# Four graph layers over 32 batches: first two batches and the last turn's last layer in halves, bias rows spread by a product, two batches kept on chip

## The chip, the cores and the metric

The kernel runs on one core of one Trainium2 chip. The metric is the time on the device in microseconds (us); a run's time is that of one launch. Times of single instructions come from one profiled execution of the kernel. In what follows PE is the matrix engine (TensorE) and PEld its loading of stationary operands, DVE is VectorE, ACT is ScalarE, POOL is GpSimd and SP is SyncE, which here only issues transfers. L1234 is line 1234 of the kernel before.

## What is computed

32 batches of a graph with 512 nodes and 128 features each, `x` (32, 512, 128), and a symmetric adjacency `adj` (32, 512, 512) of zeros and ones go through four residual layers. Every layer first takes a layer norm and a ReLU of x.

```python
h = relu(ln(x)); x = x + attention(h, adj)     # q, k, v = relu(h W + b); softmax over the neighbours; times v
h = relu(ln(x)); x = x + gcn_lstm(h, adj)      # sigmoid((A_norm h) @ lw); lw: a 3-tap convolution of the
                                               # last 128 nodes, then an LSTM of 128 steps over all batches
h = relu(ln(x)); x = x + four_layers(h, adj)   # each: tanh of ((src and dst sums over normalized adj), own) @ wu + bu,
                                               # with inputs of 1, 1, 2 and 3 blocks of 128 features
h = relu(ln(x)); x = x + prelu(adj @ (h W^T) + bias)
```

## The kernel before

Two programs stand in the kernel. `symmetric` makes the whole result if the adjacency is symmetric and the exponentials stay in range; it counts violations as it goes, and at its end each engine loads a flag and branches past `general`, which would compute everything again without those assumptions.

`symmetric` does not issue its instructions as it meets them. Each piece of work is an operation with an engine (or a choice of ACT or DVE), an estimated duration, a rank and the tiles it reads and writes. `Plan.run` (L613 to L791) simulates the engines with these estimates, takes the operation of lowest rank that can start first, and so writes an order for every engine. On the chip each engine then works through its order strictly, and waits on semaphores where its input is late. The constants at L537 to L541 and L811 to L832 feed this planner: `SWITCH` is the time it assumes for a change between whole products and products in 32-column tiles, `FIRST_GAPS`, `LANDED` and `STORED` are the times it assumes for transfers to land, `PATIENCE` and `LEAD` shift what goes first.

The work has these stages:

- Head (L959 to L987): ACT issues the loads of the attention weights, of the column biases `colb` and of the row bias R_V, broadcast to all partitions into `brow`. It then loads its function table. SP's first loads are x of the first batches. PE runs 20 warm-up products on a tile of zeros (`warm_up`, L981).
- Pass 1 (`pass_1`, L1164) goes over all batches; position 0 is the first batch that is not in `RESIDENT` (L822), and the resident batches 0, 1 and 2 come last. For each it loads x and the last 128 columns of the adjacency (`f_al`), normalizes, transposes (L902, or L1198), makes keys (`f_pk`), the query of the last 128 nodes (`f_pql`) and values (`f_pv`), and the attention of those nodes (`f_sl`, `f_pol`), which the convolution (`f_pd`) and the LSTM need. Only position 0 works in halves of two tiles each (L1182 to L1203). The value product adds to a PSUM bank that `fill` (L992) has filled with the bias. A batch that is not resident stores its keys and relu'd inputs (448 KB) and values (258 KB). The folding of the weights of the third layer's source, own and target products (`fold`, L1030) is spread among positions 2 to 5 (`FOLD_AT`).
- Pass 2 (`pass_2`, L1361) finishes the attention of the other 384 nodes, in products of 32 columns (`f_pq`, `f_s`, `f_po`), from the stored or resident tiles. The LSTM (`lstm`, L1289) runs its 128 steps through it with the highest priority.
- The rest (`rest`, L1556) is done in 32 turns, one batch each, several in flight. A turn makes the gate, then the four layers (L1640 to L1663). Each layer is a product `f_py` into a bank filled with the bias, a split of the result into a rounded part and a remainder (L1501 on ACT, L1502 on DVE), the sums over neighbours `f_pa` (8 products of 512 columns), a scaling by `f_inv` (L1654 on DVE), the own products added to the same bank (L1658), and a tanh (L1662 on ACT). After the fourth layer its result is transposed back (`f_n4T`), added to x (L1679) and normalized; then come the products with the adjacency (`f_pg`), an eviction to `f_g`, the last matrix (`f_p`, L1706) and the update: L1709 adds the positive part, L1713 and L1714 the negative one. For turns 29 and 30 L1713 and L1714 are put off behind the last turn's normalization (`put_off`, L1530).
- The last turn (turn 31): its normalization is `relu_first` (L1514): statistics of four tiles, one root on POOL (L1091), the shift, then scaling and rounding on ACT (L1525) and the remainder on DVE (L1527). The products with the adjacency run in two column halves (L1693). 16 warm-up products are interspersed (L1677). The second half's store is issued by ACT, the first's by SP (L1719). The flag's load (`read`, L1752) comes after that.

## Time and profile before

| | us |
|---|---|
| median of 3 runs | 1277.38 (1276.59 to 1277.43) |
| profiled execution, its time | 1275.34 |
| profiled execution, its span from first to last instruction | 1273.4 |
| PE busy, DVE busy, ACT busy, POOL busy | 1255.8, 985.9, 837.8, 400.7 |
| first product of the LSTM (`f_z`) | 190 |
| last product of the last turn's fourth layer | 1249.9 to 1252.6 |
| issue of the last store | 1266.87 |

The page gives busy times, but PE's busy time contains warm-up products and matmuls whose ends are modelled; an engine that is busy for 99% may still lose time to both. The chain of waits lists, in order of time, what the end depended on; its pieces are not stretched, so the work of a stretch can be summed from it. The view of stretches gives each engine's busy time in a window, with the share of the 16 DMA engines. In a timeline row the numbers are start, busy time, engine, line, operation, output from inputs and count; the brackets hold the idle time before it and what released it.

### The profile page before, as it was taken

Reading aid. Unit: us, or ns where it says so; the run is one execution under the profiler, and the core shown is the slowest. Engines: PE = TensorE matmul, PEld = TensorE weight load, DVE = VectorE, ACT = ScalarE, POOL = GpSimd, SP = SyncE. Lnnn points to the kernel's source line nnn. Section 1 sums busy time; section 2 is a strip of 40 time slices with the busy share of each in tenths; the row PEclk is TensorE's granted clock in tenths of the full one; section 3 lists DMA queues with packets and bytes.
Section 4 is the critical chain, followed back from the end, with each engine's and each line's share of the span. In section 5 each row is a group of like instructions: output and inputs, shape, how many; then the busy total and the mean of one; then the engine's idle time right before and its main releaser. Section 6 shows DMA issues by size and latency. Waiting matters only on the chain.

```text
span 1273.4 us, 33089 instructions
## 1 busy us (share of the span) xinstructions
PE 1255.8 (99%) x12074; PEld 970.9 (76%) x12075; DVE 985.9 (77%) x3275; ACT 837.8 (66%) x2102; POOL 400.7 (31%) x734
## 2 busy tenths in 40 slices
PE   9999999999999999999999999999999999999997
PEld 7988876666666767777778787787787877877775
DVE  7899869989899889775677677676776776787755
ACT  4667677778777667774576676666766766675433
POOL 3556533324233135331223233232242232332001
PEclk9999999999999999999999999999999999999999
DMA  8888887778986797876476677777777777482211
GB/s 270 255 274 277 275 270 233 213 226 272 277 259 214 213 251 210 174 175 160 83 178 156 155 173 160 153 174 152 175 154 151 175 157 153 89 174 59 50 33 37
DMA packets 313052, 232.02 MB, mean 182 GB/s; under 512 B 151601, under 2 KB 258481, under 8 KB 312881
## 3 DMA queue, kind: packets, MB, share of 16 engines
q1 hardware_dynamic: 295280, 212.65, 61.5%
q0 software_dynamic: 16896, 16.78, 8.5%
q8 instruction: 97, 1.59, 0.5%
q14 instruction: 75, 0.61, 0.2%
q10 hardware_dynamic: 704, 0.40, 0.1%
HBM read 135.73 MB, written 62.58 MB: 156 GB/s over the span
## 4 chain that ended last, share of the span: by engine, by line
PE 86%; DVE 6%; POOL 2%; ACT 2%; DMA 2%; issue 1%; SPq 0%; ACTq 0%; DVEq 0%
PE f_pa L1538 18%; PE f_py L1647 15%; PE f_pa L1658 15%; PE f_pg L1538 8%; PE f_po L1415 5%; PE f_z L1303 4%; PE f_s L1409 4%; PE f_pol L1251 2%; PE f_pk L1177 2%; PE f_p L1706 2%; PE f_sl L1241 2%; PE f_pv L1219 2%; PE f_pl L1612 2%; PE f_pd L1276 2%; PE f_pq L1399 1%; DVE f_e L1413 1%
## 5 line engine op out<-in xcount | busy, mean ns | idle before, releaser
L1538 PE MATMUL f_pa<-f_ar,f_y 128*128 128x512 f32 x1024 | 298.0, 428 | 0.2 <-ACT f_y L1501 0.2
L1538 PEld LDWEIGHTS f_pa<-f_ar,f_y 128*128 128x128 f32 x1024 | 189.3, 188 | 73.1 <-issue 38.7
L1647 PE MATMUL f_py<-f_wf,f_n 128*128 128x128 f32 x1280 | 173.7, 275 | 0.0
L1647 PEld LDWEIGHTS f_py<-f_wf,f_n 128*128 128x128 f32 x1280 | 165.0, 191 | 10.1 <-issue 2.9
L1662 ACT ACTIVATE f_n<-f_pa,f_bcol 128x512 f32<-128x512 f32 x128 | 88.3, 690 | 101.9 <-PE f_pa L1658 99.0
L1658 PE MATMUL f_pa<-f_n,f_wf 128*128 128x512 f32 x320 | 152.7, 593 | 0.1
L1456 ACT ACTIVATE f_ar<-f_a 128x512 fp32r<-128x512 f32 x224 | 138.7, 622 | 4.1 <-PE f_pg L1538 2.4
L1463 POOL DMA_DIRECT2D f_das<-f_ar x32 | 27.1, 846 | 360.2 <-ACT f_ar L1456 338.1
L1501 ACT CAST f_y<-f_py 128x512 fp32r<-128x512 f32 x128 | 75.3, 589 | 72.1 <-PE f_py L1647 65.5
L1502 DVE TENSOR_TENSOR f_y<-f_py,f_y 128x512 fp32r<-128x512 f32 x128 | 87.7, 687 | 34.9 <-ACT f_y L1501 33.4
L1654 DVE TENSOR_TENSOR f_pa<-f_pa,f_inv 128x512 f32<-128x512 f32 x128 | 86.9, 694 | 28.0 <-PE f_pa L1538 27.9
L1415 PE MATMUL f_po<-f_v,f_e 128*32 128x129 f32 x3072 | 108.0, 273 | 0.4 <-DVE f_e L1413 0.2
L1415 PEld LDWEIGHTS f_po<-f_v,f_e 128*32 128x32 f32 x3072 | 90.9, 110 | 21.1 <-issue 16.6
L1658 PEld LDWEIGHTS f_pa<-f_n,f_wf 128*128 128x128 f32 x320 | 57.9, 190 | 47.0 <-issue 42.6
L1409 PE MATMUL f_s<-f_q,f_k 128*32 128x384 f32 x928 | 92.0, 486 | 0.2 <-issue 0.2
L1303 PE MATMUL f_z<-f_w,f_seq 128*32 128x128 f32 x2040 | 83.4, 276 | 5.2 <-DVE f_seq L1349 2.3
L1303 PEld LDWEIGHTS f_z<-f_w,f_seq 128*32 128x32 f32 x2040 | 53.0, 109 | 45.1 <-ACT f_e L1412 10.0
L1132 DVE COPY f_hl_d<-f_n 128x1024 uint16<-128x1024 uint16 x27 | 18.7, 694 | 88.0 <-ACT f_n L1662 88.0
L1472 DVE SCALAR_TENSOR_TENSOR f_aT<-f_a,f_aT 128x1024 bf16<-128x1024 f32 (+1 forms) x68 | 76.3, 1152 | 0.5 <-DMA f_aT<-f_das 0.5
L1647 PE MATMUL f_py<-f_wf,f_T_c 128*128 128x128 f32 x448 | 72.8, 275 | 0.0
L1538 PE MATMUL f_pg<-f_ar,f_xp_d 128*128 128x512 f32 x248 | 71.9, 413 | 0.0
L1538 PE MATMUL f_pg<-f_ar,f_xp_c 128*128 128x512 f32 x256 | 68.4, 407 | 0.6 <-ACT f_xp_c L1509 0.4
(213 smaller groups left out, 2755.1 us busy)
## 6 DMA issues: line engine op xcount, KB each, us to landing
f_a<-in_adj_dram SPq DMA_DIRECT2D x112, 256.0 KB
f_a<-in_adj_dram SPq DMA_DIRECT2D x28, 1024.0 KB
f_das<-f_ar POOLq DMA_DIRECT2D x32, 512.0 KB, 4.8
f_dkq<-f_kh SPq DMA_DIRECT2D x29, 448.0 KB
f_al<-in_adj_dram SPq DMA_DIRECT2D x32, 256.0 KB
f_inv<-f_ddi SPq DMA_DIRECT2D x32, 256.0 KB
f_x<-in_x_dram SPq DMA_DIRECT2D x31, 256.0 KB
out_dram<-f_x SPq DMA_DIRECT2D x31, 256.0 KB
```

Of the source, the lines that this page charges most:

```text
L1303: nc.tensor.matmul(z.t[part, k, :, :], h, w[:, m : m + 4, part], start=False, stop=True, skip_group_check=True)
L1409: PE(R, t_mm(NR), lambda s=s, j=j: quarters(lambda p: nc.tensor.matmul(s.t[p], keys_of()[:, j * P + p.start : j * P + p.stop], q_of(), sta ...
L1415: PE(R, t_mm(P), lambda e=e, t=t, j=j: quarters(lambda p: nc.tensor.matmul(po.t[p, t, :], e.t[:, t * P + p.start : t * P + p.stop], v.t[:, ...
L1456: ACT(rank, 0.62, lambda t=t: nc.scalar.activation(ar.t[:, t, :], a.t[:, t, :], AF.Square, accum_out=deg.t[:, t : t + 1]), [(a, t)], [(ar, ...
L1472: nc.vector.scalar_tensor_tensor(flat(aT.t[:, n * k : n * (k + 1), :]), flat(a.t[:, n * k : n * (k + 1), :]), 1.0, flat(aT.t[:, n * k : n ...
L1501: ACT(rank, t_act(N), lambda: nc.scalar.copy(parts.t[:, :, 0, :], src.t), [src], [(parts, 0)])
L1502: DVE(rank, t_dve(N), lambda: nc.vector.tensor_sub(parts.t[:, :, 1, :], src.t, f32(parts.t[:, :, 0, :])), [src, (parts, 0)], [(parts, 1)])
L1538: nc.tensor.matmul(pg.t, parts.t[:, j, k, :], ar.t[:, j, :], start=(k == 0 and j == 0), stop=(k == 1 and j == NT - 1))
L1647: nc.tensor.matmul(py.t[:, j, :], nodes[n].t[:, bass.ts(j, P)], wf[:, W_F[i] + c, 0, :], start=False, stop=(c == nch - 1), skip_group_chec ...
L1654: before = DVE(R, t_dve(N), lambda pa=pa: nc.vector.tensor_mul(pa.t, pa.t, inv_row.t), [inv_row], [pa])
L1658: nc.tensor.matmul(pa.t, wf[:, W_F[i] + c, 1, :], nodes[n].t, start=False, stop=(c == nch - 1), skip_group_check=True)
L1662: ACT(R, 0.57, lambda pa=pa, n=n, i=i: nc.scalar.activation(n.t, pa.t, AF.Tanh, bias=bcol[:, i : i + 1]), [pa], [n])
```

## The change

The parts, in the order of the program:

1. Constants of the planner: `SWITCH`, `FIRST_GAPS`, `LEAD`, `STORED`, `PATIENCE`, `FOLD_AT`; one operation (the flag's load) gets an earlier rank.
2. `RESIDENT` is two batches, not three.
3. Loads of the head: column biases first, then the function table, then the attention weights. The rows R_V and R_CONV are loaded as one row into partition 0 of a zeroed 128 x 256 tile (part of the LSTM's sequence tile), and a product with a matrix of ones spreads them to all partitions; ACT copies them out. The two broadcast loads go. The convolution's weights are loaded later. 17 warm-ups, not 20.
4. Pass 1: x of the first three positions is loaded ahead of the rest; positions 0 and 1 (`HALVED` = 2) work in halves of two tiles; position 0's fill with the value bias is for ACT only.
5. The last turn: the fourth layer (`BY_HALVES` = (3,)) by halves of two tiles (`layer_by_halves`), the transposing back and adding by halves (`update_by_halves`), the normalization's statistics and root by halves (`relu_first`); 4 + 3 warm-ups, not 16.
6. L1709 of a put-off turn is put off too; for turn 30 (`WAITING`) it waits for the last turn's remainders; L1713 comes after L1709.
7. The flag is loaded after the last eviction of `f_g`, not after the last store's issue.

```diff
-    SWITCH = (0.28, 0.1)
+    SWITCH = (0.25, 0.12)
...
-                first = self.lead if sub == 4 else 0.0
+                first = self.lead if sub == 4 else 60.0 if sub == 3 else 0.0
...
-    FOLD_AT = (2, 3, 4, 5)
+    FOLD_AT = (3, 4, 5, 6)
...
-    RESIDENT = range(3)
-    FIRST_GAPS = (2.0, 2.8, 3.0, 3.5)
-    LEAD = 0.0
+    RESIDENT = range(2)
+    FIRST_GAPS = (2.0, 3.5, 4.0, 4.0)
+    LEAD = 3.0
...
-    STORED = 3.0
-    PATIENCE = 1.3
+    STORED = 3.5
+    PATIENCE = 1.1
...
-    load_beside(w[:, :W_CONV, :], weights[:, :W_CONV, :], w_att, 3.5)
     load_beside(colb, cols, w_cols, 3.0)
-    load_beside(brow[:, BR_V, :], rows[R_V].partition_broadcast(P), (biases, BR_V), 3.0)
     ACT(HEAD, 1.5, lambda: nc.scalar.activation(table, neg_half[:, 0, 0:1], AF.Exp))
-    w_conv = load(HEAD + 12, 192, w[:, W_CONV:W_IH, :], weights[:, W_CONV:W_IH, :])
-    w_crow = load(HEAD + 12, 64, conv_row, rows[R_CONV].partition_broadcast(P))
+    load_beside(w[:, :W_CONV, :], weights[:, :W_CONV, :], w_att, 3.0)
+    two_rows = flat(seq[:, : 2 * P // B, :])
+    nc.vector.memset(two_rows, 0.0)
+    w_rows = plan.fixed(two_rows)
+    load_beside(two_rows[0:1], rows[R_V : R_CONV + 1].rearrange("(o r) f -> o (r f)", o=1), w_rows, 2.5)
+    w_conv = load(HEAD + 22, 192, w[:, W_CONV:W_IH, :], weights[:, W_CONV:W_IH, :])
+    w_crow = plan.fixed(conv_row)
...
-    for k in range(20):
+    for k in range(17):
...
+    spread = bank("f_spread", (P, 2, P), whole=False)
+    PE(HEAD, t_mm(2 * P), lambda: nc.tensor.matmul(flat(spread.t), ones, two_rows, start=True, stop=True), [w_rows], [spread])
+    ACT(HEAD, t_act(P), lambda: nc.scalar.copy(brow[:, BR_V, :], spread.t[:, 0, :]), [spread], [(biases, BR_V)])
+    ACT(HEAD + 11, t_act(P), lambda: nc.scalar.copy(conv_row, spread.t[:, 1, :]), [spread], [w_crow])
...
-        n = 2 if pos == 0 else NT
+        n = 2 if pos < HALVED else NT
...
-            DMA(R, 64 * n, lambda at=at: nc.sync.dma_start(xc.t[:, at : at + n, :], ...
+            DMA(R if pos > 2 else HEAD + pos, 64 * n, lambda at=at: nc.sync.dma_start(xc.t[:, at : at + n, :], ...
...
-        fill(R, lambda: pv.t, bias(BR_V), [(biases, BR_V)], pv, [turned])
+        fill(R, lambda: pv.t, bias(BR_V), [(biases, BR_V)], pv, [turned], pos == 0)
...
     def relu_first(rank, xc, name):
+        for at in range(0, NT, HALF):
+            tiles = range(at, at + HALF)
+            mv = ln_stats(rank, xc, tiles, f"{name}_{at}")
+            ln_rstd(rank, mv, at, at + HALF, (lambda rs=rs, at=at: rs.t[:, at : at + HALF], rs), True)
+            for t in tiles:
+                DVE(rank, t_dve(P), lambda t=t, mv=mv: nc.vector.tensor_scalar(y.t[:, t, :], ...
...
+    def layer_by_halves(R, b, i, nodes, ar, inv_row, before):
...
+        for at in range(0, NT, HALF):
+            cols = slice(at * P, (at + HALF) * P)
+            pa = bank(f"f_pa_{b}_{i}_{at}", (P, HALF * P), whole=False)
+            for k in range(2):
+                for half in range(0, NT, HALF):
+                    def quarter(pa=pa, cols=cols, k=k, half=half):
+                        for j in range(half, half + HALF):
+                            nc.tensor.matmul(pa.t, parts.t[:, j, k, :], ar.t[:, j, cols], ...
...
+            before = DVE(R, t_dve(HALF * P), lambda pa=pa, cols=cols: nc.vector.tensor_mul(pa.t, pa.t, inv_row.t[:, cols]), ...
+            PE(R, nch * t_mm(HALF * P), own, [nodes[m] for m in CHUNKS[i]], [pa])
+            ACT(R, t_act(HALF * P) + 0.1, lambda pa=pa, cols=cols: nc.scalar.activation(n.t[:, cols], pa.t, AF.Tanh, ...
...
+            if turn == B - 1 and i in BY_HALVES:
+                before = layer_by_halves(R + 4, b, i, nodes, ar, inv_row, before)
+                continue
...
-            for k in range(2 * BUFS["mm"]):
+            for k in range(4 if two else 7):
                 warm_up(R - 4, 0.216, f"f_warm_{k}_{b}", [end4])
...
-            evict(R, n * P, lambda cols=cols: g3.t[:, cols], lambda p3a=p3a: p3a.t, [p3a], [(g3, at)])
+            late.append(evict(R, n * P, lambda cols=cols: g3.t[:, cols], lambda p3a=p3a: p3a.t, [p3a], [(g3, at)]))
+            for k in range(3 if at else 0):
+                warm_up(R - 4, 0.216, f"f_warm_{k}_{at}_{b}", [agg3])
...
+                up = DVE(R, t_dve(n * P), lambda: nc.vector.scalar_tensor_tensor(
+                    flat(xc.t[:, part, :]), flat(p3.t), 0.0, ...), [p3], mine, after=split if turn in WAITING else ())
-                ACT(R, t_act(n * P), lambda: nc.scalar.activation(neg.t[:, part, :], p3.t, AF.Relu, scale=-1.0), [p3], [(neg, at)], after=turned)
+                ACT(R, t_act(n * P), lambda: nc.scalar.activation(neg.t[:, part, :], p3.t, AF.Relu, scale=-1.0), [p3], [(neg, at)], after=list(turned) + [up])
...
-        PE(R + 4, 0.1, read, [], [], after=[said] + late)
+        PE(R + 3, 0.1, read, [], [], after=[said] + late)
```

## The prediction

> **What bounds the kernel now.** I read the page's busy table first, then the busy time by stretch, then the two ends in order of time.
>
> ```profile
> PE 1255.8 (99%) x12074; PEld 970.9 (76%) x12075; DVE 985.9 (77%) x3275; ACT 837.8 (66%) x2102; POOL 400.7 (31%) x734
> ...
> 0.00:7.45 7.45, 6.26 (x21) 2.51 (x21) 3.40 (x19) 1.49 (x2) 2.51 (x14) 1.00 0.71 181
> 7.45:14.02 6.57, 5.01 (x35) 3.92 (x33) 5.37 (x25) 3.14 (x8) 1.78 (x3) 1.00 0.94 311
> ...
> 14.00:190.00 176.00, 175.26 (x1496) 153.59 (x1496) 148.80 (x652) 119.26 (x257) 92.11 (x232) 1.00 0.85 273
> 190.00:515.00 325.00, 318.76 (x6460) 225.63 (x6461) 292.19 (x1205) 241.59 (x845) 108.23 (x193) 1.00 0.82 236
> 515.00:1254.50 739.50, 739.08 (x3995) 576.25 (x3994) 525.57 (x1346) 465.66 (x977) 195.03 (x292) 1.00 0.64 139
> 1254.50:1267.30 12.80, 11.45 (x73) 8.97 (x72) 10.55 (x31) 6.66 (x16) 1.07 (x1) 1.00 0.21 63
> ```
>
> A row holds the stretch, its length, then busy time of PE, PEld, DVE, ACT and POOL, clock, DMA share and GB/s. From 14 to 1254.5 us PE is busy for 1233.1 of 1240.5 us. The time is therefore PE's work, which the change leaves almost as it is, plus what PE loses. It loses a head, a few us in the LSTM stretch (6.2), and a tail. PE busy flatters both ends, because warm-up products count as busy. The head, in order of time:
>
> ```profile
> 1.19 6.42 PE L984 MATMUL f_warm<-f_marks 128*128 128x512 bf16 x20 [1.19 <-DVE f_marks L922]
> ...
> 5.96 0.60 DVE L1192 TENSOR_SCALAR f_xn_a<-f_x,f_mv_a,f_rs_a 128x128 f32<-128x128 f32 x2 [0.21 <-POOL f_rs_a L1091]
> ...
> 7.45 0.60 PE L1198 MATMUL f_xt_a<-f_ident,f_xn_a 128*128 128x128 f32 x4
> ...
> 8.39 0.69 DVE L1004 COPY f_pv<-f_brow 128x512 f32<-128x512 f32 x1
> ...
> 10.70 0.48 DVE L1081 BATCH_NORM_STATS2 f_st_a<-f_x 128x6 f32<-128x128 f32 x2 [1.17 <-DMA f_x<-in_x_dram]
> ...
> 11.71 1.13 PE L1241 MATMUL f_sl<-f_ql,f_kh 128*128 128x128 f32 x8 [0.75 <-DVE f_sh_a L1112]
> ```
>
> The first two normalized tiles are there at 6.56, but PE's queue still holds warm-ups and the transposes start at 7.45. Later DVE stands 1.17 us for the third batch's x (issued at 4.39, landed at 10.67 by the chain of waits), and the eviction of the second half of the first batch's keys (L1180 at 11.10) is queued behind it, so the scores wait. Real work in 7.45 to 14.02, by the chain's spacings, is transposes 0.44, keys 0.86, query 0.22, values 0.89, scores 0.89, second batch's transposes 0.44, a weight's transposes 0.33: 4.07 of 6.57 us. PE gives away 2.5 us there and the whole 7.45 before. The tail:
>
> ```profile
> 1255.22 0.60 PE L902 MATMUL f_n4T<-f_ident,f_n 128*128 128x128 f32 x4
> ...
> 1256.59 0.68 DVE L1679 SCALAR_TENSOR_TENSOR f_x<-f_n4T,f_x 128x512 f32<-128x512 f32 x1
> ...
> 1258.86 1.07 POOL L1091 TENSOR_TENSOR f_rs_d<-f_rs_d,f_neg_half 128x4 f32<-128x4 f32 x1 [6.30 <-ACT f_p L1000]
> ...
> 1260.35 0.69 DVE L1709 SCALAR_TENSOR_TENSOR f_x<-f_p,f_x 128x512 f32<-128x512 f32 x1 [0.39 <-PE f_p L1706]
> ...
> 1260.96 1.13 DVE L1527 SCALAR_TENSOR_TENSOR f_xp_d<-f_yr_d,f_rs_d,f_xp_d 128x128 fp32r<-128x128 f32 x4
> ```
>
> The last turn's tanh ends at 1253.37 and its first product of the last layer (L1693) starts at 1260.75: 7.4 us of transposing, adding, statistics, root and relu. The chain of waits shows what PE did meanwhile that is no work: f_warm pieces of 0.59, 0.86, 0.23, 0.23 and 1.09 us, 3.0 in all. After the last store each engine loads the flag and branches:
>
> ```profile
> L1753 SPq TENSOR_LOAD <-fail x1: 485/485/485, 1266.8 to 1266.8; - x1
> ...
> L1801 SPq EVENT_SEMAPHORE  x8: 17/17/17, 1270.4 to 1271.7; - x8
> ```
>
> **What the Trainium skill says.** "Runtime: NRT & Kernel Launch", Instruction fetch mechanics: a taken branch out of the fetched window stalls on a fetch. The trace agrees: SP branches at 1267.4 and its next instruction is at 1270.4. The change does not remove this. "VectorE: DVE Perf Modes", the TRN2 errata: each instruction pays a fixed cost, so halves cost more than half; here a DVE add of 512 columns takes 0.69 us and of 256 columns 0.42 to 0.44. "DMA: Bandwidth & Descriptors", Issuing engines are not separate DMA queues: all queues share 16 engines, so an earlier request takes bandwidth from its neighbours; the share of 0.94 in 7.45 to 14.02 agrees. "TensorE: Matmul & The Clock Gate", Part 1: the clock is full only after about 3.4 us of activity; the trace's warm-ups are why there are 17 left and not none.
>
> **Head.** Three warm-ups less are 3 x 0.216 = 0.65 us (the planner's price; the later warm-ups' rows have this spacing); the transposes' inputs are there at 6.56, so they can take it. Adds a 256-column fp32 product (half of the 0.86 of a 512-column one: 0.43) between warm-ups and transposes; it lies in PE time otherwise idle if the row has landed, and costs up to 0.43 if not. The three first x transfers now go ahead of the adjacency columns, of the convolution's 192 KB and of its 64 KB row: the third x leaves SP fifth, at about 2.8, not at 4.39. Ahead of it are then 512 KB of x and 192 KB of weights; before, another 512 KB besides. I let it land by about 7.5, so that DVE's 1.17 us wait goes; of it 0.8 is on PE's path (scores at 11.71, their query ready at 10.5). The fill of 0.69 at 8.39 leaves DVE for ACT, which idles 1.58 us there: 0.3 for the first keys' eviction. The second batch in halves starts keys after two tiles: its eviction of 0.59 becomes two of 0.33 to 0.38 on ACT, which has room (3.14 of 6.57 busy); gain 0.25. Sum 0.65 + 0.8 + 0.3 + 0.25 = 2.0 us. What may take it back: the attention weights go out after the table load (1.28 + 0.20), at 2.75 instead of 0.74; with the same 3.25 us to land they come at 6.0, and the keys want them at about 7.6. If they need 6 us as the third x did, 1.2 us are lost. Bounds: loss of 0.5 to gain of 3.3.
>
> **Tail.** Own products and aggregation of the last turn's fourth layer are cut in columns: 8 products of 512 columns (0.23) become 16 of 256 (L1693's sixteen show 0.118 unstalled), 6 fp32 passes of 0.43 become 12 of 0.215; PE's work is equal. What shrinks is the chain behind the last product: tanh 0.69 to 0.4, transposes 0.44 to 0.22, add 0.68 to 0.42, statistics 1.23 to 0.6, root 1.07 to about 0.95: 1.5 us shorter for the second half, the first ahead by 1.3. Besides, transposes no longer queue behind other turns (1253.6 possible, 1255.22 real; the raised priority), nor the add behind L1714 (0.7). PE has 0.93 + 1.85 + 0.44 + 2 x 0.89 = 5.0 us of work to lay under a chain of some 4 to 5 us, so most of 0.59 + 0.86 should go: 1.2; and 0.3 of the 0.46 lost between products of L1693, as the tiles' parts come earlier. The 1.09 between last product and last matrix stays: evictions were in halves already. Putting turn 30's L1709 (0.69 at 1260.35, just ahead of L1527) behind the split helps those parts, but it then stands with L1714 twice (2 x 0.7) in the 2 us before the last L1709: minus 0.3. The flag's load moves to between eviction and last product, where PE, ACT and SP idle over 0.5 us; SP then branches 0.5 earlier, and its chain of semaphore instructions ends the span: 0.5. DVE's load (0.54) is in the minus 0.3. Sum 1.2 + 0.3 + 0.5 - 0.3 = 1.7. Bounds: loss of 0.5 (DVE becomes the bound there) to gain of 3.5.
>
> **Middle.** Two batches stay instead of three. Stored again: 448 + 258 KB; read again: 192 + 256 + 258 + 192 + 64 = 962 KB; with 273 and 236 GB/s 2.6 and 4.1 us of DMA time, at shares of 0.85 and 0.82, beside PE. I set it at nothing: this batch is now the first of pass 1 and its stores lie some 170 us ahead of the reads. The folds' one position later, and the planner's constants (switching 0.28/0.1 to 0.25/0.12, patience 1.3 to 1.1, store 3.0 to 3.5), shuffle the order between 14 and 515; the trace cannot say which way. Bounds plus or minus 1.5, taken 0. From 515 to 1254.5 PE idles 0.4 us; nothing to gain.
>
> **Sum.** 2.0 + 1.7 = 3.7. Against the profiled execution: 1275.34 (span 1273.4, 1.9 around it) minus 3.7 is 1271.6. The median of the runs shown is 2.0 above that execution, so the forecast for a median is 1277.4 - 3.7 = 1273.7.
>
> **Rivals.** (1) One end only: weights or the bias row land late and the head keeps its idle time, or the tail's DVE, busy 10.55 of 12.8 us there, becomes its bound. For it: a DMA share of 1.00 from 5 to 10 us. Against: 2.5 us of plain gaps. Gives 1277.4 - 1.7 = 1275.7. (2) The reshuffled LSTM stretch gains too: of its 6.2 idle us 2 to 4 go; 1277.4 - 3.7 - 3 = 1270.7. Nothing but those gaps speaks for it. (3) Slower: the third batch's absence starves PE where pass 1 ends. From 176 to 200 us PE fills its gaps with the batches kept on chip (f_s<-f_q,f_kh, 96 products, first at 176.6). A batch has (108.0 + 92.0 + 9.3 + 23.9 + 2.5) / 32 = 7.4 us of this work by the page's groups. If its reloads queue behind adjacency at a DMA share of 0.84, PE stands up to 7.4: 1277.4 - 3.7 + 7.4 = 1281.1. It decides from a loss of 3.7 + 2.6 = 6.3 us on. Against it: the longest gap there is 0.5 us (before f_z at 190), and two other batches' work comes first.
>
> **Numbers.** A measurement of this kernel can tell about 0.2%, 2.6 us, from no change. Forecast 0.55, rival 1 0.22, rival 2 0.08, rival 3 0.15. Faster 0.63, same 0.22, slower 0.15. The forecast's own range is 1271 to 1275; with the bounds (3.3 + 3.5 + 1.5 = 8.3 of gain at most, 2.5 of loss) and part of rival 3 the range is 1269.5 to 1279.8.
>
> **What would show it.** Right: first transposes before 7.0; no DVE wait of a us for x before 12; the state of 14.02 (scores done, second batch's keys begun) by 12; less than 1.5 us of warm-ups in the tail's chain; flag loads ahead of the last L1709, SP's next instruction after its branch about 0.5 us sooner against the store. Wrong: keys waiting for f_w; DVE back to back from L1527 to the last L1714; PE gaps of over 1 us between 176 and 215.

## The result and the profile after

The changed kernel takes 1279.69 us (median of 22 runs, 1277.48 to 1284.24) against 1276.57 us for the kernel before beside it: ratio 1.0021, 95% interval 1.0014 to 1.0028. By the ratio it is 2.7 us slower, where 3.7 us less were forecast. The profiled execution has a span of 1278.3 us against 1273.4.

The page's busy line of the changed kernel, and then its busy time in the stretches that the prediction used:

```profile
PE 1256.5 (98%) x12081; PEld 975.2 (76%) x12081; DVE 981.2 (77%) x3282; ACT 826.8 (65%) x2107; POOL 387.8 (30%) x736
```

```profile
7.45:14.02 6.57, 6.10 (x40) 4.78 (x39) 6.53 (x34) 4.81 (x13) 2.71 (x4) 1.00 1.09 346
14.00:190.00 176.00, 172.53 (x1417) 151.39 (x1419) 148.55 (x645) 112.12 (x240) 88.52 (x229) 1.00 0.84 269
190.00:515.00 325.00, 316.13 (x6531) 226.16 (x6524) 287.66 (x1186) 240.36 (x843) 104.87 (x190) 1.00 0.80 237
515.00:1254.50 739.50, 738.48 (x3981) 575.54 (x3980) 520.61 (x1354) 458.14 (x990) 186.04 (x295) 1.00 0.63 141
```

TensorE's total is the same (1256.5 for 1255.8), so the loss is not new work. Its first stretch here is fuller, 6.10 of 6.57 us for 5.01: the head did what it should. The next two are emptier: 3.5 us idle from 14 to 190 where 0.7 were, and 8.9 from 190 to 515 where 6.2 were. That is 5.4 us in the part that I had set at nothing.

The head in order of time, TensorE's rows:

```profile
1.18 6.40 PE L991 MATMUL f_warm<-f_marks 128*128 128x512 bf16 x17 [1.18 <-DVE f_marks L926]
7.42 0.59 PE L997 MATMUL f_spread<-f_seq,f_ones 128*128 128x256 f32 x2
7.85 0.60 PE L1210 MATMUL f_xt_a<-f_ident,f_xn_a 128*128 128x128 f32 x4
...
11.02 1.06 PE L1253 MATMUL f_sl<-f_ql,f_kh 128*128 128x128 f32 x8
...
12.13 1.38 PE L1189 MATMUL f_pk<-f_kh,f_w 128*128 128x256 f32 x4
```

Seventeen warm-ups take as long here as twenty did (6.42), and the transposes start 0.4 us later than before. Yet the scores start at 11.02 for 11.71, and VectorE's wait for the third batch's x is gone (its waits for x are now 1.39 and 1.73 us, at 2.94 and 5.38, for the first batch's halves). The second batch's keys begin at 12.13 for 14.02; 0.33 of these 1.9 us is a weight's transposing, which now comes later. To compare the two at equal work I summed TensorE's products at their unstalled price and noted when both kernels reach the same sum. This is an estimate, good to half a us or so: the lead is between 1.5 and 2.0 us at 14 us and under 1 us at 100 us, and at 111 us it has become a lag of about 2.

The tail, by the chain of waits (start, length, group, number of instructions):

```profile
1266.14 0.67 PE f_warm L991 x3
1266.81 0.89 PE f_p L1791 x8
1267.70 2.01 PE f_pg L1776 x16
1269.71 0.88 PE f_warm L991 x4
1270.59 0.96 PE f_p L1791 x8
```

There are 1.55 us of warm-ups where 3.0 were. The aggregation's sixteen products run through in 2.01 us; before, they took from 1261.11 to 1263.45, 2.34 us with warm-ups between them. And after the last store, by the instructions of the flag's line and of the branch's:

```profile
L1835 SPq TENSOR_LOAD <-fail x1: 477/477/477, 1269.7 to 1269.7; - x1
...
L1883 SPq EVENT_SEMAPHORE  x8: 17/17/17, 1276.0 to 1276.6; - x8
```

The load stands ahead of the end (1269.7, with the last addition at 1272.46), and from the start of the last store at 1272.97 to the end of the span there are 5.3 us, for 6.5 before (1266.87 to 1273.4). SP's next instruction after its branch comes 3.0 us after the store's start for 3.5, and its eight semaphore instructions are spread over 0.6 us for 1.3.

So both ends are shorter and the middle is longer. What made the middle longer is the question of the experiments. Two places stand out in the trace. At 104 us GpSimd waits for a load of 128 numbers:

```profile
100.66 0.21 POOL L1278 MEMSET f_hp<- 128x130 f32 x1 [1.58 <-PE f_pd L1288]
104.21 0.24 POOL L985 TENSOR_SCALAR f_minus_alpha<-f_alpha 128x1 f32<-128x1 f32 x1 [3.35 <-DMA f_alpha<-in_prelu_a_dram]
104.40 0.10 POOL L1224 MEMSET f_v<- 128x4 f32 x1
104.58 0.24 POOL L1102 TENSOR_SCALAR f_rs_a<-f_mv_a 128x4 f32<-128x4 f32 x1
```

The product with minus one is needed more than 400 us later, but GpSimd keeps its order: the root of a batch's statistics (L1102) is behind it. TensorE's rows show who pays:

```profile
105.83 0.66 PE L906 MATMUL f_xt_a<-f_ident,f_xn_a 128*128 128x128 f32 x4 [1.39 <-DVE f_ql L1192]
106.32 1.06 PE L1263 MATMUL f_pol<-f_v,f_el 128*128 128x129 f32 x8
108.21 0.91 PE L1288 MATMUL f_pd<-f_w,f_hp 128*128 128x128 f32 x6 [0.83 <-ACT f_pv L1012]
```

2.2 us of gaps in one place. Before, GpSimd's product with alpha stood at 116.3 us and made nobody wait:

```profile
L978 POOL TENSOR_SCALAR f_minus_alpha<-f_alpha x1: 250/250/250, 116.3 to 116.3; 128x1 f32<-128x1 f32 x1
```

The other place is spread over the LSTM; here is one step of it in the changed kernel, in order of time and with the other engines' work left out:

```profile
367.10 0.19 ACT L1353 ACTIVATE f_th<-f_z 128x32 f32<-128x32 f32 x1
...
367.57 0.20 POOL L1452 TENSOR_TENSOR f_rs<-f_ln,f_d 128x4 f32<-128x4 f32 x1
...
367.81 0.16 DVE L1124 SCALAR_TENSOR_TENSOR f_sh_c<-f_ln,f_rs 128x4 f32<-128x4 f32 x1 [0.44 <-POOL f_rs L1452]
367.89 0.22 DVE L1347 SCALAR_TENSOR_TENSOR f_cu<-f_th 128x64 f32<-128x64 f32 x1
...
368.92 0.21 DVE L1361 STREAM_TRANSPOSE f_seq<-f_h 128x32 f32<-128x32 f32 x1
...
369.27 0.64 PE L1315 MATMUL f_z<-f_w,f_seq 128*32 128x128 f32 x16 [1.28 <-ACT f_ar L1468]
```

The gates are there at 367.29, but VectorE has a normalization of another batch (L1124) ahead of the cell's update (L1347), and that one waits 0.44 us for GpSimd. The step's state arrives at 369.13, and TensorE, which has the next step's products at the head of its queue and nothing before them, has stood for 1.28 us. The bracket names f_ar, which was done at 369.17; f_seq, 0.04 us earlier, is the step's own chain. A step of the LSTM costs TensorE nothing as long as enough other products are queued between its parts; how many stand there is decided by the planned order.

### The profile page after: what moved, and what is told of

Its sections match the earlier page's. It is cut to its first block, busy times and chain, and to the rows that moved or that the text cites. A ratio compares the mean times of both kernels' runs of the same rounds, so it can differ in the third digit from the quotient of the medians.

```text
span 1278.3 us, 33162 instructions
## 1 busy us (share of the span) xinstructions
PE 1256.5 (98%) x12081; PEld 975.2 (76%) x12081; DVE 981.2 (77%) x3282; ACT 826.8 (65%) x2107; POOL 387.8 (30%) x736
## 4 chain that ended last, share of the span: by engine, by line
PE 86%; DVE 6%; ACT 2%; DMA 2%; POOL 2%; issue 1%; ACTq 0%; DVEq 0%
PE f_pa L1555 18%; PE f_py L1726 15%; PE f_pa L1737 15%; PE f_pg L1555 8%; PE f_po L1427 4%; PE f_z L1315 3%; PE f_s L1421 3%; PE f_pl L1688 2%; PE f_p L1791 2%; PE f_pk L1189 2%; PE f_sl L1253 2%; PE f_pol L1263 2%; PE f_pv L1231 2%; PE f_pd L1288 2%; DVE f_e L1425 1%
## 5 line engine op out<-in xcount | busy, mean ns | idle before, releaser
L1726 PEld LDWEIGHTS f_py<-f_wf,f_n 128*128 128x128 f32 x1264 | 162.4, 191 | 9.7 <-ACT f_n L1741 1.6
L1427 PE MATMUL f_po<-f_v,f_e 128*32 128x129 f32 x3072 | 112.8, 273 | 0.0
L1427 PEld LDWEIGHTS f_po<-f_v,f_e 128*32 128x32 f32 x3072 | 94.1, 110 | 21.8 <-issue 17.3
L1421 PE MATMUL f_s<-f_q,f_k 128*32 128x384 f32 x960 | 96.5, 486 | 0.2 <-issue 0.2
```

What stands on the lines that cost most here:

```text
L1421: PE(R, t_mm(NR), lambda s=s, j=j: quarters(lambda p: nc.tensor.matmul(s.t[p], keys_of()[:, j * P + p.start : j * P + p.stop], q_of(), sta ...
L1427: PE(R, t_mm(P), lambda e=e, t=t, j=j: quarters(lambda p: nc.tensor.matmul(po.t[p, t, :], e.t[:, t * P + p.start : t * P + p.stop], v.t[:, ...
L1726: nc.tensor.matmul(py.t[:, j, :], nodes[n].t[:, bass.ts(j, P)], wf[:, W_F[i] + c, 0, :], start=False, stop=(c == nch - 1), skip_group_chec ...
```

## The experiments

The theories: A, the ends gain what was forecast and something in the middle loses it, be it the third batch (A1), the planner's constants (A2) or the load of alpha (A3). B, the parts of the ends themselves disturb what is behind them. C, it hardly matters what is edited: any edit that the planner sees gives another plan of the LSTM stretch (its order, and which of ScalarE and VectorE does a piece of work that either can do), and any other plan is worse than that of the kernel before.

Each kernel was compared with the kernel before beside it, whose median is 1275.9 to 1277.0 in the four sets of runs; so the ratios are what compares. The table has the median, the ratio with its interval, the span of the profiled execution, TensorE's busy time in the 325 us from 190 to 515, and a mark: the start of the twentieth f_neg (L1713 before), some 250 us before the end. The mark compares only kernels with the old tail: the new one puts f_neg behind L1709, and with it alone the mark is 3.2 us later while the end is 2.3 us earlier. Span, busy time and mark are of one execution each.

```
kernel                      median   ratio   interval          span    190-515  mark
before                      1276.57  1                         1273.4  318.76   1017.3
changed                     1279.69  1.0021  1.0014 to 1.0028  1278.3  316.13   1027.5
changed, three stay         1278.49  1.0009  1.0000 to 1.0018  1275.2  314.76   1025.0
changed, old constants      1284.12  1.0051  1.0032 to 1.0070  1284.5  311.80   1033.6
changed, alpha planned      1278.50  1.0009  1.0001 to 1.0018  1274.7  316.38   1024.2
before + both ends          1279.04  1.0018  1.0008 to 1.0029  1278.4  313.99   1028.1
before + tail               1274.58  0.9979  0.9969 to 0.9990  1271.1  318.14   1020.5
before + head               1281.76  1.0038  1.0024 to 1.0051  1278.0  315.60   1021.7
before + two stay           1283.86  1.0054  1.0039 to 1.0070  1281.8  314.04   1025.6
before + constants          1285.62  1.0074  1.0057 to 1.0091  1282.4  313.55   1025.4
before + 1 ns, LSTM price   1279.93  1.0030  1.0022 to 1.0037  1276.8  315.91   1020.6
before + 1 ns, ACT price    1285.68  1.0071  1.0054 to 1.0089  1284.0  309.47   1027.2
before + tail + warm-ups    1274.28  0.9986  0.9977 to 0.9995  1270.4  318.75   1019.5
  and x and fill            1272.87  0.9970  0.9961 to 0.9980  1274.9  317.71   1024.7
```

**Three batches stay.** In the changed kernel:

```
-    RESIDENT = range(2)
+    RESIDENT = range(3)
```

> The changed kernel with three batches kept on chip again (RESIDENT = range(3)), all else as changed. Theory A1 (the loss sits in the middle and comes from the batch that is no longer kept, by its stores and reloads and by the missing filler work): about 6 us less than the changed kernel, some 1273.5. Theory A2 (it comes from the planner's constants): within 1.5 us of the changed kernel, and the LSTM stretch's gaps stay. Theory A3 (it comes from the multiplication L985 that stands on POOL for its transfer at 104 us): no change beyond 1.5 us unless that multiplication happens to move; if it moves, about 2 us less. Theory C (every edit shuffles the planner's order by some us, whatever it is): any value within plus or minus 4 us, not tied to the stretch where the third batch works.

1.5 us less than the changed kernel (1.0009 for 1.0021); by its interval it is between level with the kernel before and 2.3 us over it. A1's 6 us are not there. The LSTM stretch is even emptier (314.76), and the wait at 104 us is shorter because alpha landed sooner in this execution: 5.2 us from its issue to the product, for 6.9 in the changed kernel.

**The old constants.** In the changed kernel:

```
-    SWITCH = (0.25, 0.12)
+    SWITCH = (0.28, 0.1)
...
-    STORED = 3.5
-    PATIENCE = 1.1
+    STORED = 3.0
+    PATIENCE = 1.3
```

> The changed kernel with the planner's constants of before (SWITCH 0.28 and 0.1, PATIENCE 1.3, STORED 3.0), all else as changed. Theory A2: about 5 to 6 us less than the changed kernel, switches between tiled and untiled products back from 28 to about 34, and the gaps between 190 and 515 us back from 9 to about 6 us. Theory A1: within 1.5 us of the changed kernel. Theory A3: within 1.5 us unless L985 moves. Theory C: anything within plus or minus 4 us.

A2 fails with the sign turned: the old constants cost 3.8 us more in this order.

**Alpha's load with its real time.** In the changed kernel:

```
-    w_alpha = load(LAST, 1, alpha, prelu_a.partition_broadcast(P))
+    w_alpha = plan.fixed(alpha)
+    DMA(LAST, 1, lambda: nc.sync.dma_start(alpha, prelu_a.partition_broadcast(P)), [], [w_alpha], gap=8.0)
```

> The changed kernel with one number more: the planner is told that the load of alpha takes 8 us to land, not 2. The multiplication L985 is then put on POOL well after its transfer has landed. Theory A3: the 3.35 us that POOL stands at 104 us go, with them PE's 1.39 and 0.83 us gaps there, and the whole is 2 us or more less than the changed kernel; if the delay at 104 us was also what upset the LSTM stretch, up to 6 less. Theories A1 and A2: at most 2 us less. Theory C: the gaps at 104 us go, but the total moves by anything within plus or minus 4 us since the planner's later order moves too.

TensorE's order of instructions is that of the changed kernel to the last row. On GpSimd the product is now at 110 us, behind the root that it had held up, and waits for nothing:

```profile
110.03 0.25 POOL L986 TENSOR_SCALAR f_minus_alpha<-f_alpha 128x1 f32<-128x1 f32 x1
```

```profile
95.00:115.00 20.00, 20.00 (x156) 17.99 (x156) 19.32 (x88) 13.30 (x27) 11.83 (x32) 1.00 0.87 258
```

The second fence is the busy time from 95 to 115 us: TensorE is never idle there, where it was for 2.2 of 20 us. The whole gains 1.5 us by the ratios (1.0021 to 1.0009, with intervals that overlap a little), less than A3 wanted, and the LSTM stretch stays as empty as it was (316.38 for 316.13), as is to be expected with the same order.

**Both ends on the kernel before.** The changes of head and tail, with three batches kept and the old constants, on the kernel before (the diff is the change's without these two settings).

> The kernel before with both ends of the change (loads and their order, spread bias rows, two batches in halves, fewer warm-ups, the folds one position later; last turn in halves with its priorities and the flag's earlier load), but with three batches kept and the planner's old constants. Theory A (ends gain what was forecast, the middle's two settings lose it): 3 to 4 us less than the kernel before, about 1273. Theory B (the ends' own parts disturb the stretch behind them): like the changed kernel, 2 to 4 us more than before, with the loss already there at 130 us. Theory C: anything from 4 less to 3 more, with head and tail shorter by about 2 us each in the trace.

2.3 us over the kernel before: theory A falls. The two settings of the middle do not carry the loss; without them it is the same. B and C both allow this result.

**Each part alone.** Four kernels, each the kernel before with one part of the change: its tail; its head; one line of two batches kept; the three constants.

```
-    RESIDENT = range(3)
+    RESIDENT = range(2)
```

> The kernel before with the tail of the change alone (last turn's fourth layer, update and statistics in halves, its priorities, fewer warm-ups there, the flag's earlier load). The order of TensorE's instructions is that of the kernel before up to the end of the LSTM. Theory of the ends (the tail's step stands): 1.5 to 2.5 us less than before, ratio about 0.9985, all of it behind 1250 us. Theory of the shuffle (any edit moves the planned order and costs 2 to 4 us on the way): not less than before, with the difference already there at 600 us.

> The kernel before with the head of the change alone (loads and their order, spread bias rows, two batches in halves, 17 warm-ups, the folds one position later), three batches kept, old constants, old tail. Theory B (the head's parts disturb what is behind them): 3 to 5 us more than before, ratio 1.0025 to 1.004: 2 to 3 less at 14 us, 2.5 given back at 104 us where POOL stands for alpha, and 4 to 5 lost between 190 and 515 us. If only the sum of both ends disturbs the LSTM stretch: 1 to 2 us less than before.

> The kernel before with two batches kept on chip in place of three, nothing else. As a cost by itself (stores, reloads, missing filler work): 2 us or more over before, with gaps of PE where pass 1 ends. As a mere shuffle of the order: anything within plus or minus 3 us, the difference arising within the LSTM stretch and not where the third batch is worked on. As the run with three batches in the changed kernel suggests (1 us less with three): about 1 us over before.

> The kernel before with the change's planner constants alone. If they are better as such, as in the changed kernel, where the old ones cost 4 us: 2 to 4 us less than before. If constants only fit the order they were picked for (the shuffle): 1 to 5 us more than before, arising between 190 and 515 us.

The tail alone gains 2.7 us, the only part that gains, and the only one that leaves the order of TensorE's instructions as it was up to the LSTM's end. The head alone loses 4.8 us, the two batches 6.9, the constants 9.4. At equal work the tail alone is level with the kernel before, within 0.3 us, at 1250 us, so its gain is the tail's own. The constants' loss is beyond what any theory had put down (5 at most), that of two batches beyond the 3 us of the shuffle; the other theory's sign for it, gaps where pass 1 ends, is not there. The parts do not add up: the four make -2.7 + 4.8 + 6.9 + 9.4 = 18.4, and together they lose 2.7.

Where the other three lose is the same for all. By the mark, head alone is behind by 4.4 us at 1017 and by 4.6 at the end; two batches by 8.3 and 8.4; constants by 8.1 and 9.0. So next to nothing is lost in the last 250 us. At equal work two batches kept are level with the kernel before, within 0.3 us, at 243 us; nearly all comes between 250 and 600. In the head alone alpha had landed earlier, with the same order on GpSimd around it as in the changed kernel:

```profile
101.82 0.24 POOL L982 TENSOR_SCALAR f_minus_alpha<-f_alpha 128x1 f32<-128x1 f32 x1 [1.36 <-DMA f_alpha<-in_prelu_a_dram]
```

A wait of 1.36 us costs TensorE nothing, one of 3.35 us costs 2.2. The kernel with both ends has the head's plan on every engine up to the LSTM's end, and in its execution GpSimd waited 3.5 us. TensorE's busy time from 95 to 115 us, in the head alone and then with both ends:

```profile
95.00:115.00 20.00, 19.98 (x154) 17.80 (x153) 19.10 (x91) 13.90 (x28) 11.38 (x31) 1.00 0.82 252
```

```profile
95.00:115.00 20.00, 17.68 (x131) 15.31 (x131) 16.82 (x74) 11.59 (x24) 10.58 (x28) 1.00 0.75 233
```

The same instructions thus pay 2.3 us in one execution and nothing in another, which fits a median that gained 1.5 and not 2.2.

**A nanosecond.** Two kernels whose only edit is a number that the planner reckons with, and that no instruction carries:

```
-    T_STEP = 0.22
+    T_STEP = 0.221
```

```
-        return 0.17 + n * 0.0006
+        return 0.171 + n * 0.0006
```

> The kernel before with one planner price changed by 1 ns: T_STEP, what the planner thinks a group of recurrent products takes, 0.221 for 0.22. No instruction is added or removed by it as such; only the planned order moves (386 rows of TensorE's order differ, all between the end of pass 1 and soon after the LSTM). Theory of the shuffle (the order of before is a lucky one, and any other costs some us): 1 to 6 us more than before. Theory that the change's own parts cost the time: within 1 us of before.

> The kernel before with another planner price changed by 1 ns: 0.171 for 0.17, what the planner thinks an operation of ScalarE takes at least. Only the order moves (627 rows of TensorE's order, from pass 1 on). Theory of the shuffle: 1 to 6 us more than before, lost between 190 and 515 us. Theory that the change's own parts cost the time: within 1 us of before.

3.8 and 9.1 us over the kernel before, the second more than the 6 us that even the theory of the shuffle allowed. This decides for C: there is no new work, no transfer moved on purpose and no constant retuned, and the loss is as large as that of the change's parts. What such an edit changes is the plan, and that is more than TensorE's order: some evictions change engine too (by the pages ScalarE has 2112 instructions and VectorE 3265 with the LSTM's price raised, 2099 and 3278 with ScalarE's, 2102 and 3275 before). What each of the two costs alone was not tried. The busy time from 190 to 515 us, with the LSTM's price and then with ScalarE's price raised; before, TensorE's 325 us had 318.76 busy:

```profile
190.00:515.00 325.00, 315.91 (x6421) 221.62 (x6422) 289.01 (x1194) 237.86 (x833) 106.09 (x191) 1.00 0.78 232
```

```profile
190.00:515.00 325.00, 309.47 (x6327) 217.50 (x6320) 285.32 (x1169) 232.49 (x818) 99.97 (x181) 1.00 0.76 228
```

TensorE loses 2.9 and 9.3 us more there than before, close to the whole loss. Its waits for the recurrent state in the same stretch (total, times, longest), with the same two prices, with the constants alone, the head alone, and in the changed kernel:

```profile
PE f_z L1303 <- DVE f_seq L1349: 5.5, 13, 1.3
```

```profile
PE f_z L1303 <- DVE f_seq L1349: 9.2, 17, 1.6
```

```profile
PE f_z L1303 <- DVE f_seq L1349: 5.2, 17, 0.7
```

```profile
PE f_z L1312 <- DVE f_seq L1358: 5.1, 12, 1.2
```

```profile
PE f_z L1315 <- DVE f_seq L1361: 3.5, 13, 0.7
```

And in the kernel before, in the tail alone, which has its order there, and in the changed kernel with alpha planned:

```profile
PE f_z L1303 <- DVE f_seq L1349: 2.3, 7, 0.6
```

```profile
PE f_z L1306 <- DVE f_seq L1352: 2.6, 8, 0.6
```

```profile
PE f_z L1316 <- DVE f_seq L1362: 2.5, 11, 0.5
```

This one line does not rank the orders: the changed order has 3.5 us of it in one execution and 2.5 in the other. TensorE's whole idle time does. From 190 to 515 us it is 6.2 to 7.3 us in the four executions with the order of the kernel before, and 8.6 to 15.5 in the ten with another; two executions of one order differ by up to 1.6. In the two kernels with a nanosecond changed most of what is added is the wait for the recurrent state; with the constants alone it is not only that (see the last section). The LSTM itself is no longer in the changed kernel than before. By the rows of its products (durations, then first and last start), in the kernel before and in the changed one:

```profile
L1303 PE MATMUL f_z<-f_w,f_seq x2040: 269/273/298, 185.1 to 491.3; 128*32 128x128 f32 x186
```

```profile
L1315 PE MATMUL f_z<-f_w,f_seq x2040: 269/273/298, 188.0 to 494.4; 128*32 128x128 f32 x186
```

306.2 and 306.4 us (the table ahead has 190 for the first product; by this row it is 185.1). The worst of the nanoseconds, ScalarE's, has 306.1; over all kernels it is 304.6 to 309.6. So what is lost is in the main other work that could have been done beside it: it is left over and done later.

**The gains without the order.** The tail, and of the head only what can be had without the planner noticing. First three warm-ups fewer, with the later ones priced higher, so that the planner's sum stays:

```
-    for k in range(20):
-        warm_up(HEAD, 0.43 if k < 8 else 0.216, f"f_warm_{k}")
+    for k in range(17):
+        warm_up(HEAD, 0.43 if k < 8 else 0.288, f"f_warm_{k}")
```

> The kernel before with the tail of the change, and 17 warm-up products for 20, the later nine priced at 0.288 in place of 0.216, so that the planner sees the same total and its order stays: apart from three products fewer every engine's order is that of the kernel with the tail alone. If the term of the warm-ups stands (3 times 0.216): 0.65 us less than with the tail alone, ratio about 0.9975 to before. If the clock warms up later with fewer products, or the inputs are what is late: no less than with the tail alone, 0.998.

0.9986, its interval overlapping that of the tail alone (0.9979): no gain of fewer warm-ups can be told, but the intervals, 1.1 us to either side, are too wide to tell 0.65 us. Then, besides, the first fill of values on ScalarE alone, and the third batch's x put ahead of the adjacency's columns by hand, once the plan is made:

```
+            if pos < 3:
+                plan.first.append(o)
...
         self.order = order
+        for k, o in enumerate(self.first[2:]):
+            o.start = self.first[1].start + 0.01 * (k + 1)
```

> As the last, and with two more parts of the head that leave the order of everything else as it was: the first fill of values goes to ScalarE, and the third batch's x is issued ahead of the adjacency's columns (its place in the order is set by hand after planning). If the ends bring what was forecast as long as the order in the middle stays: 3 to 4.5 us less than before, ratio 0.9965 to 0.9975, with TensorE 1.5 to 2.5 us ahead at 20 us and still 1 or more ahead at 500. If pass 1 is bound by its transfers, so that a head start there is given back: not more than 0.5 us less than with the tail alone, 0.998.

0.9970, interval 0.9961 to 0.9980: 3.8 us less than the kernel before. It beats both kernels. That this is nearly the 3.7 us forecast for the whole change is a coincidence, as its parts are others. Over tail and warm-ups it gains 1.4 us in the median (1272.87 for 1274.28), which is not clear of noise: the two intervals overlap a little, and that of the tail alone overlaps it widely. The two signs expected of the trace are not there: its profiled execution, 4 us over the kernel's median, is 2.2 us behind the kernel before at 20 us. VectorE waits for the second batch's x, which probably lands later because the third's is now under way with it, and has it ahead of the first batch's second half (VectorE's row, then TensorE's):

```profile
9.06 0.49 DVE L1087 BATCH_NORM_STATS2 f_st_a<-f_x 128x6 f32<-128x128 f32 x2 [2.53 <-DMA f_x<-in_x_dram]
```

```profile
9.94 0.49 PE L1206 MATMUL f_xt_a<-f_ident,f_xn_a 128*128 128x128 f32 x2 [3.03 <-DVE f_xn_a L1200]
10.27 1.86 PE L1185 MATMUL f_pk<-f_kh,f_w 128*128 128x256 f32 x4
```

The second thing to see here is the last row: the keys' four products take 1.86 us where they took 1.13 before. After the gap of 3.03 us the granted clock of this trace is 0.50 from 11 to 14 us. How often all this happens a single trace cannot say. That the gain over tail and warm-ups comes from an earlier start is therefore argued and not shown.

One thing this trace does show. It is 2.4 us behind the kernel before at the first scores of pass 1 (`f_sl`, 14.1 for 11.7 us) and still 2.4 behind at the last (178.5 for 176.1): as long as the order is kept, pass 1 neither makes up nor loses time. In the new order it does: the head alone is 0.9 us ahead at the first and 0.5 behind at the last (176.6), and alpha planned 1.7 and then 1.2 ahead (10.0 and 174.9). In neither did TensorE lose time to alpha's load.

Not tried: the head's other parts (the second batch in halves, the spread bias rows, the order of ScalarE's loads) with the order of the kernel before. What they are worth there is open.

## Why the prediction was wrong, point by point

The step that failed is the middle: "shuffle the order between 14 and 515; the trace cannot say which way. Bounds plus or minus 1.5, taken 0". The sentence is right and both numbers are wrong. Ten of the kernels here have another order of the LSTM stretch than the kernel before, eight different orders in all (alpha planned has that of the changed kernel, and both ends that of the head alone), and none has as much of TensorE's time from 190 to 515 us as it. Edits that touch nothing but the plan cost 3.8 and 9.1 us. The order of the kernel before is the best of all those seen, so by them the mean of a shuffle is not 0: it had to be taken as a loss, here of some 4 to 9 us, as large as what the ends can give or larger. Why that order is so good no run shows. The profile did hold a hint: 2.3 us of waiting for f_seq in 128 steps. A step takes 306.2 / 128 = 2.4 us; where TensorE has next to nothing else queued, the chain from one step's products to the next takes 2.05 (377.09 to 379.14 in the kernel with ScalarE's price raised, with a wait of 1.22 at its end). So there is little idle time left between the steps, and another order has little to gain and much to lose.

For the changed kernel the sum is, by the ratios: tail -2.7 (tail alone); the wait for alpha +1.5 (with and without it); the head some -2.0 at 14 us, by its one trace; so that 2.7 + 2.7 - 1.5 + 2.0 = 5.9 us remain for the new order, the head start that pass 1 gave back included. This is a remainder and not a measurement: it takes medians, one trace and three intervals of about 1 us together. The settings and constants of the middle are draws of the same lot: the new constants cost 9.4 us in the order of before and gain 3.8 in that of the changed ends.

- **Head, -2.0.** At 14 us the size is about right, but it hangs on the clock, and the lead did not last. The second batch's keys began 1.9 us earlier (2.9 with alpha planned, at 11.16), and DVE's wait for the third batch was gone. The 0.65 for three warm-ups is hidden by the clock. The warm-ups follow each other at 0.43 us first and at 0.216 later (the rows of PEld show the spacing), and the change comes at 5.00 us in the kernel before, at 6.28 in the changed one and anywhere from 3.7 to 6.7 us in the 14 executions. Twenty warm-ups took 6.4 to 7.3 us in six of them and seventeen took 5.1 to 6.4 in eight: fewer do end sooner, but the changed kernel's execution, with a late change of clock, is the longest of the eight (6.40), and that with alpha planned is among the short ones (5.22). The transposes came at 7.85 and 6.67 in these two, so "before 7.0" held in some executions and not in that of the changed kernel. The Trainium skill, "TensorE: Matmul & The Clock Gate", Part 1, says that the warm-up is a stretch of time and not a number of products, and that its window runs free, so that the change of clock moves by 500 ns either way. The first agrees with the runs: 6 to 13 products were slow. The 500 ns do not: the change came 2.5 to 5.5 us after the first product. I had cited the page for why warm-ups are there, and took the moment of the change as given. Keys did not wait for their weights. What the step leaves out is that the lead has to last: in the head alone it was gone by the end of pass 1.
- **Tail, -1.7.** Right, and if anything too small: 2.7 alone, by interval 1.3 to 4.0. In the changed kernel's trace the warm-ups went from 3.0 to 1.55 (forecast 1.2 of it), the sixteen products are 0.33 shorter (0.3), and from the last store to the end there are 1.2 us less where 0.5 were put down for the flag's load: 0.5 is the earlier branch, as forecast, and 0.7 the shorter row of semaphore instructions, which was not forecast. The 1.09 between last product and last matrix became 0.88. The fear of VectorE as a bound had some ground: it is busy from 1263.2 to 1269.2 with one gap of 0.23 us, and the 0.67 of warm-ups that are left fall into this time.
- **The load of alpha** is in none of my steps. I did not ask what the planner moves by itself, and past whom: GpSimd's product with alpha (L978) went from 116 to 104 us and stands ahead of a root that TensorE needs soon.
- **Rival 3** has the right sign and the wrong mechanism. No gap over 0.7 us stands between 176 and 215, and two batches alone are level with the kernel before at 243 us. It is not the third batch that is missed where pass 1 ends; the cost of keeping two comes later, in the order that this gives. Whether the reloads beside the LSTM have a part in it no run separates.
- **Rivals 1 and 2**: both ends gained, and the LSTM stretch lost.
- **The chances.** I gave a loss 0.15, because I priced the ends in tenths and the order with a symmetric guess. The one large unknown should have set the chances. That the 1279.69 us still lie within my outer range (to 1279.8) is no merit: its upper end came from rival 3, whose mechanism is not what happened.

## What to carry to other kernels

Where a planner or a hand-made order fills the gaps of a long recurrent chain, every edit upstream is two edits: what it does, and a new draw of the order. A kernel that was kept because it measured well may hold a lucky draw, so that most others are worse. Price the draw first: change one of the planner's numbers by a nanosecond and measure, which gave 4 and 9 us here. Then bring a gain in without the planner noticing (a padded price, a transfer moved after planning), and compare the two orders of instructions before believing in a difference.

A load that nobody needs for a long time still blocks the queue in which its first user stands. Tell the planner a time to land near the longest that was seen, not the usual one (here 8 us for 2).

## What the runs showed that was not expected

The same transfer of 0.5 KB for alpha, issued into transfers that are busy for about 0.8 of the time, landed 4.9, 5.2, 6.9, 6.9 and 7.0 us after the start of its issue in five executions (issue at 96.94, 96.27, 97.35, 96.17 and 97.49; the waiting product at 101.82, 101.5, 104.21, 103.1 and 104.5). Those 2 us decide whether TensorE pays.

TensorE sometimes stands in the middle of one line's products with nothing to wait for, as here in the kernel with the constants alone ("issue" means that the profile shows no releaser):

```profile
452.48 1.30 PE L1415 MATMUL f_po<-f_v,f_e 128*32 128x129 f32 x36
455.92 0.30 PE L1415 MATMUL f_po<-f_v,f_e 128*32 128x129 f32 x2 [2.13 <-issue]
```

After it the granted clock is 0.57 from 457 to 461 us, as it was halved after the gap of 3.03 us in the head of the kernel with x and fill; in the other twelve traces it stays at 1.00 between head and tail, in that with both ends too, which has a gap of 2.25 us at 415. So 2.1 us of the 9.0 that the constants lose in this execution are that gap, and some 1.7 more (an estimate from the clock: 0.43 of 4 us) the slower products behind it. These are not waits for the recurrent state.

In the tail alone and in tail with warm-ups such a gap, of 0.8 and 1.1 us, stands at 313 and 311 us; the kernel before with the same order has none there. The Trainium skill, "Runtime: NRT & Kernel Launch", Instruction fetch mechanics, says that an engine streams its instructions in blocks and that crossing from one to the next is mostly hidden; whether these gaps are what isn't hidden, no run here shows. It was not tried and stays open.
